# Layer 0's attention weights from image pairs (t, t+d): 17 differences instead of all 32 partners

## The chip, the cores and the metric

One core of one Trainium2 chip. The metric is the device time of one execution, in microseconds (us). Five runs of the kernel before the change lie between 3171.18 and 3187.57 us, median 3178.15 us. Everything is fp32.

## What is computed

The reference runs two layers on `x` of shape (4, 32, 128, 128). Layer 0 is a spectral-convolution attention over the 32 images of each of the 4 batches; layer 1 (pairwise attention over 1024 tokens and a mixture of experts) fills the rest of the time and is not touched. Cut to what matters, layer 0 is:

```
xn = inorm(group_norm(x))
k, q = fno_layer(xn, Kcw, Ksw, 64, 64), fno_layer(xn, Qcw, Qsw, 64, 64)   # 32 heads
v    = fno_layer(xn, Vcw, Vsw, 128, 128)
scores[b, n, t, s] = sum_k qf[b, n, t, k] * kf[b, n, s, k] / 64
p_attn = softmax(scores, axis=-1)             # 32 x 32 for each of 32 heads
av = p_attn @ v ; p = fno_layer(av, Pcw, Psw) ; norms, a two-layer fno, residuals
```

Keys and queries are spectral layers of one image each, so a score is a weighted sum, over the kept frequencies, of products of the two images' Fourier coefficients: for each head n, `w_re[mode, n]` times Re(X_t X_s*) and `w_im[mode, n]` times Im(X_t X_s*). The real part is the same for (t, s) and (s, t), the imaginary part changes sign.

## The kernel before, in words

**Spectra.** `spectra_of_images` turns the 32 images of a batch into `xx[p, t, y]`: 128 partitions are 64 row frequencies, real parts in the lower half, imaginary parts in the upper half; y counts column frequencies. ACT then copies the 17 kept column frequencies into `xm[p, 2*17, t]` (L457, two copies of 128x544 that turn t and y around): plane yy is the spectrum, plane 17+yy the spectrum with its halves turned and signed, so that a product of the two gives the imaginary part.

**Attention weights.** `attention_weights(b, front)` runs once per batch, four times in all, and is the only large piece that the change touches. Its steps in order:

- ACT copies the 17 planes into `xp` in PSUM (L495), so that DVE reads one operand from PSUM.
- PE sums the frequencies above 17, which all heads share, in `so[t, s]` (32x32; 15 pairs of L503, then L504); DVE spreads it on a diagonal as `sod` (32x1024, L506).
- For each of the 17 planes yy there are two outer products over t and s, each 128x1024: `pa` (real part) on DVE, `pb` (imaginary part) on DVE for every third plane (L522) and on POOL for the others (L524): 22 on DVE and 12 on POOL. PE contracts each over its 128 partitions, with `w_re` or `w_im` as stationary 128x32, in two halves of 512 columns (L528): four products per plane, one on each quarter of the 128 PSUM partitions of `sp`. A fp32 matmul shows as two records.
- ACT copies `sp` (128x512) to `spt` (L536). PE adds four terms into `sc` (64 x 32 x 16: two halves of t on partitions): `qk` by `sod` (L540) and `halves` by `spt` (L547), each for two halves.
- Softmax: DVE maximum (L558), DVE difference (L559), ACT Exp (L560), DVE sum (L562), reciprocal (L563), DVE product (L564). The result `ph` goes out to DRAM and comes back as `pr` in another layout (L572, L577).

**Buffers.** `sod`, `pa`, `pb`, `ph`, and later the `u` tiles share one tag `pr` with six buffers. `xp`, `so`, `sc`, and later the tiles `y1` and `xw`, share the PSUM tag `wide` with two buffers.

**What runs around it.** In layer 0 the order of each engine's work is decided by the framework's scheduler; each engine then runs its own list in order. For batch 0 the stage stands alone, with some setup on DVE behind it (L649 to L684). For batches 1 to 3 it overlaps the end of the batch before: ACT scales 32 images (L999), POOL adds them in four pieces (L1006), and after the stage PE and DVE run `back` (L297, L308) and the last residual (L1010). The next batch begins with `cm` (L703), and with `po` (L778), the products of `pr` with `u = xb*gb` (L773 on POOL, L775 on DVE).

Of the kernel before, what the change touches and what calls it, by code (L numbers as in the profile page):

```python
# [7 lines left out]
F32 = mybir.dt.float32  # L8
AF = mybir.ActivationFunctionType
ALU = mybir.AluOpType  # L10
# [3 lines left out]
P = 128  # L14
# [21 lines left out]
def _constants():  # L36

    w = np.arange(P)
    kx = np.concatenate([np.arange(32), np.arange(-32, 0)])
    ky = np.arange(KY)  # L40
    th = 2 * np.pi / P
    c, s = np.cos(th * np.outer(w, kx)), np.sin(th * np.outer(w, kx))
    rows = np.concatenate([c, -s], 1)
    inv_rows = np.concatenate([c.T, -s.T], 0)
    angle = th * np.outer(w, ky)
    cc, cs = np.cos(angle), np.sin(angle)

    cols1 = np.concatenate([cc[:, 32:33], cs, cc], 1) / NPIX
    cols2 = np.concatenate([0 * cc[:, :1], -cc, cs], 1) / NPIX
    along_c = np.concatenate([cc[:, 1:], cs[:, 1:], -cs[:, 1:]], 1) / NPIX  # L50
    twice = np.where(ky == 0, 1.0, 2.0)[:, None]
    re, im = twice * cc.T, -twice * cs.T
    inv_cols = np.concatenate([re, im], 0)
    back = np.tile(2 * np.concatenate([cc.T[1:], cs.T[1:]], 1), (4, 1))
    p = np.arange(P)
    same = (p[:, None] % 32 == np.arange(32)[None, :]).astype(np.float64)
    block = (p[:, None] // 32 == np.arange(4)[None, :]).astype(np.float64)

    eye = np.eye(32)
    comb = np.zeros((4, 32, 3, 32))  # L60
    comb[0, :, 0], comb[3, :, 0] = eye, -eye
    comb[1, :, 1], comb[2, :, 1] = eye, eye
    comb[:, :, 2] = -comb[:, :, 0]
    halves = np.concatenate([np.eye(64), np.eye(64)], 0)

    group = (p[:, None] // 4 == p[None, :] // 4) / (4.0 * NPIX / C * T)
    of_group = p[:, None] // 4 == np.arange(32)[None, :]
    by_p = np.concatenate(
        [rows, inv_rows, cols1, cols2, same, block, comb.reshape(P, 96), halves, group, of_group / 4]
        + [along_c, back],  # L70
        1,
    )
    return by_p.astype(np.float32), inv_cols.astype(np.float32)
# [35 lines left out]
def layer0(  # L109
# [37 lines left out]
    inv = columns(128)  # L147
    cols1, cols2 = columns(NX), columns(NX)
    same, block = columns(32), columns(4)
    comb, halves, group, of_group = columns(96), columns(64), columns(P), columns(32)  # L150
    cos_c, sin_c, minus_sin_c = columns(NY), columns(NY), columns(NY)
    cos_back, sin_back = columns(P), columns(P)
    par = const.tile([P, NSMALL], F32, name="par")
    nc.sync.dma_start(out=par, in_=small_row.partition_broadcast(P))
    ident = const.tile([P, P], F32, name="ident")
    make_identity(nc, ident)
    mean_w = const.tile([P, P], F32, name="mean_w")
    nc.vector.memset(mean_w, 0.5 / P)
    one_of_8 = const.tile([P, 39], F32, name="one_of_8")
    nc.vector.memset(one_of_8, 0.0)  # L160
    nc.vector.memset(one_of_8[:, 7:8], 1.0)
# [41 lines left out]

    def inv_std(name, var, n=T):

        ve, r, t = (one(f"{name}{k}", n) for k in ("_ve", "", "_t"))
        nc.vector.tensor_scalar(ve, var, 1e-5, None, ALU.add)
        nc.scalar.activation(r, ve, AF.Ln)
        nc.scalar.activation(r, r, AF.Exp, scale=-0.5)
        nc.vector.tensor_mul(t, r, r)  # L210
        nc.vector.tensor_mul(t, t, ve)
        nc.vector.tensor_scalar(t, t, -0.5, 1.5, ALU.mult, ALU.add)
        nc.vector.tensor_mul(r, r, t)
        return r, ve

    def stats(name, st):
# [9 lines left out]
        )  # L226
        nc.vector.tensor_tensor(pk[:, 1], pk[:, 1], sq[:, :, 1], ALU.add)
        m = ps.tile([P, 2, T], F32, name="m", tag="wide")
        nc.tensor.matmul(m, mean_w, pk, start=True, stop=True)
        mean, var = per_image(f"{name}_mean"), per_image(f"{name}_var")  # L230
        nc.vector.tensor_copy(mean, m[:, 0])
        nc.vector.tensor_mul(var, mean, mean)
        nc.vector.tensor_tensor(var, m[:, 1], var, ALU.subtract)

        x0 = ps.tile([P, 2, T], F32, name="x0", tag="wide")
        nc.tensor.matmul(x0[:, 0], rows, pk[:, 0], start=True, stop=True)
# [181 lines left out]
    def spectra_of_images(b, xt, normed):  # L418
# [33 lines left out]
        nc.vector.memset(xx[96:97, :, 0], 0.0)  # L452


        xm = modes.tile([P, 2 * KA, T], F32, name=f"xm_{b}", tag="xm")
        for k, y0 in enumerate((1 + KY, 1)):
            nc.scalar.copy(  # L457
                xm[:, k * KA : (k + 1) * KA], xx[:, :, y0 : y0 + KA].rearrange("p t y -> p y t")
            )
        return xx, xm, xd  # L460

    def value_weights():
        t1, t2 = (prep.tile([NH, KX, KA], F32, name=f"v{n}", tag=f"t{n}") for n in (1, 2))
# [7 lines left out]
        for ri, (b, d, op) in enumerate(  # L471
# [9 lines left out]
            for k in range(2):  # L481
# [2 lines left out]
                    in_=gd[ri, 16 * k : 16 * k + 16].unsqueeze(0).to_broadcast([8, 16, NM]),  # L484
                )

    def attention_weights(b, front):

        xx, xm, _ = front
        xs = per_image("xs")  # L490
        nc.vector.tensor_copy(xs, xx[:, :, 0])

        xp = ps.tile([P, KA, T], F32, name="xp", tag="wide")
        for y0, n in ((0, 16), (16, 1)):
            nc.scalar.copy(xp[:, y0 : y0 + n], xm[:, y0 : y0 + n])  # L495


        tt = [P, T, T]
        so = ps.tile([T, T], F32, name="so", tag="wide")
        xh = per_image("xh")  # L500
        nc.vector.tensor_scalar(xh, xs, 0.5, None, ALU.mult)
        for yy in range(KA, 32):
            nc.tensor.matmul(so, xx[:, :, 1 + KY + yy], xx[:, :, 1 + KY + yy], start=yy == KA, stop=False)  # L503
        nc.tensor.matmul(so, xh, xs, start=False, stop=True)  # L504
        sod = grp.tile([T, T, T], F32, name="sod", tag="pr", bufs=6)
        nc.vector.tensor_tensor(  # L506
            sod,
            ident[:T, :T].unsqueeze(2).to_broadcast([T, T, T]),
            so.unsqueeze(1).to_broadcast([T, T, T]),
            ALU.mult,  # L510
        )

        sp = ps.tile([P, T, 16], F32, name="sp", tag="b")
        for yy in range(KA):
            xs_p = xp[:, yy].unsqueeze(2).to_broadcast(tt)
            xs_s = xm[:, yy].unsqueeze(2).to_broadcast(tt)
            pa = grp.tile(tt, F32, name="pa", tag="pr", bufs=6)
            pb = grp.tile(tt, F32, name="pb", tag="pr", bufs=6)
            for k, t in enumerate((pa, pb)):
                other = xm[:, k * KA + yy].unsqueeze(1).to_broadcast(tt)  # L520
                if k == 0 or yy % 3 == 2:
                    nc.vector.tensor_tensor(t, xs_p, other, ALU.mult)  # L522
                else:
                    nc.gpsimd.tensor_tensor(t, xs_s, other, ALU.mult)  # L524
            for j, (wt, pp, h) in enumerate(
                (w, p, h) for w, p in ((w_re, pa), (w_im, pb)) for h in range(2)
            ):
                nc.tensor.matmul(  # L528
                    sp[32 * j : 32 * j + 32],
                    wt[:, yy],  # L530
                    pp[:, :, 16 * h : 16 * h + 16],
                    start=yy == 0,
                    stop=yy == KA - 1,
                )
        spt = grp.tile([P, T, 16], F32, name="spt", tag="v", bufs=3)
        nc.scalar.copy(spt, sp)  # L536
        nn = [2 * NH, T, 16]
        sc = ps.tile(nn, F32, name="sc", tag="wide")
        for h in range(2):
            nc.tensor.matmul(  # L540
                sc[32 * h : 32 * h + 32],
                qk,
                sod[:, :, 16 * h : 16 * h + 16],
                start=True,
                stop=False,
            )
            nc.tensor.matmul(  # L547
                sc[32 * h : 32 * h + 32],
                halves[:, 32 * h : 32 * h + 32],
                spt,  # L550
                start=False,
                stop=True,
            )


        ph = grp.tile(nn, F32, name="ph", tag="pr", bufs=6)
        mx = small.tile([2 * NH, 16], F32, name="mx", tag="mx")
        nc.vector.tensor_reduce(mx, sc.rearrange("n s t -> n t s"), AX.X, ALU.max)  # L558
        nc.vector.tensor_tensor(ph, sc, mx.unsqueeze(1).to_broadcast(nn), ALU.subtract)  # L559
        nc.scalar.activation(ph, ph, AF.Exp)  # L560
        sm = small.tile([2 * NH, 16], F32, name="sm", tag="mx")
        nc.vector.tensor_reduce(sm, ph.rearrange("n s t -> n t s"), AX.X, ALU.add)  # L562
        nc.vector.reciprocal(sm, sm)  # L563
        nc.vector.tensor_tensor(ph, ph, sm.unsqueeze(1).to_broadcast(nn), ALU.mult)  # L564

        prd = dram.tile([2, T, 16, T], F32, name=f"prd_{b}")
        pr = big.tile([P, 4, 2, T], F32, name=f"pr_{b}", tag="prob")
        for k in range(2):
            for h in range(2):
                eng = nc.scalar if h else nc.sync  # L570
                p0 = 32 * h + 16 * k
                eng.dma_start(  # L572
                    out=prd[k, :, :, 16 * h : 16 * h + 16].rearrange("s n t -> n s t"),
                    in_=ph[p0 : p0 + 16],
                )
            eng = nc.scalar if k else nc.sync
            eng.dma_start(  # L577
                out=pr[:, :, k], in_=prd[k].rearrange("(i s) n t -> (s n) i t", i=4)
            )
        return ph, pr  # L580
# [1065 lines left out]
```

## Time and profile before

| | |
|---|---|
| median of 5 runs | 3178.15 us |
| the profiled execution's own time | 3182.88 us |
| its span, first to last instruction | 3181.2 us |
| PE / DVE / ACT / POOL busy, share of the span | 92% / 72% / 73% / 66% |
| mean granted TensorE clock | 0.956 |
| layer 0 | about the first 1100 us; layer 1 begins to overlap it near the end |

The four attention stages, in us from the span's start:

| batch | first product (L522) | last contraction ends (L528) | `ph` ready (L564) | first `po` (L778) |
|---|---|---|---|---|
| 0 | 72.37 | 99.45 | 110.77 | 115.91 |
| 1 | 311.79 | 345.28 | 353.15 | 375.45 |
| 2 | 570.65 | 604.26 | 612.13 | 633.43 |
| 3 | 830.60 | 864.08 | 871.95 | 890.03 |

How to read the views: a group's row gives engine, operation, what it writes and reads, shape and count, then the mean time of one. In the chain of waits each piece is start, length and what ran, followed back from the last instruction to what released it; "issue" is time in which the profile shows no wait. In a table of stretches, PEclk is the granted TensorE clock as a share of full speed.

### The profile page before, as it was taken

Reading aid. Unit: us, or ns where it says so; the run is one execution under the profiler, and the core shown is the slowest. Engines: PE = TensorE matmul, PEld = TensorE weight load, DVE = VectorE, ACT = ScalarE, POOL = GpSimd, SP = SyncE. Lnnn points to the kernel's source line nnn. Section 1 sums busy time; section 2 is a strip of 40 time slices with the busy share of each in tenths; the row PEclk is TensorE's granted clock in tenths of the full one; section 3 lists DMA queues with packets and bytes.
Section 4 is the critical chain, followed back from the end, with each engine's and each line's share of the span. In section 5 each row is a group of like instructions: output and inputs, shape, how many; then the busy total and the mean of one; then the engine's idle time right before and its main releaser. Section 6 shows DMA issues by size and latency. Waiting matters only on the chain.

```text
span 3181.2 us, 53099 instructions
## 1 busy us (share of the span) xinstructions
PE 2920.5 (92%) x19634; PEld 1431.4 (45%) x19634; DVE 2290.3 (72%) x5035; ACT 2310.2 (73%) x3138; POOL 2102.3 (66%) x1831
## 2 busy tenths in 40 slices
PE   7889798798888789999999999999999999999997
PEld 5366266355446444443344444444444444444443
DVE  5876667667677466777666868866778777777887
ACT  2334244254353589998999999998999999999992
POOL 0721540460461389878788797889878889888773
PEclk6998899899898799999999999999999999999998
DMA  6301310230140211010111010011010011101000
GB/s 140 108 22 30 89 56 8 55 112 1 31 129 2 61 27 31 8 30 7 31 37 24 14 24 14 8 41 31 21 34 4 14 37 24 37 1 31 14 14 14
DMA packets 152309, 112.77 MB, mean 35 GB/s; under 512 B 36879, under 2 KB 140658, under 8 KB 151442
## 3 DMA queue, kind: packets, MB, share of 16 engines
q1 hardware_dynamic: 136209, 103.61, 12.2%
q10 hardware_dynamic: 15840, 5.77, 0.8%
q8 instruction: 155, 2.54, 0.3%
q14 instruction: 105, 0.85, 0.1%
HBM read 68.37 MB, written 20.00 MB: 28 GB/s over the span
## 4 chain that ended last, share of the span: by engine, by line
PE 59%; POOL 13%; DVE 9%; ACT 9%; issue 8%; DMA 1%; ACTq 0%; POOLq 0%; DVEq 0%; SPq 0%
PE d L1446 18%; PE po L1465 10%; PE px L1352 6%; ACT r L1496 4%; PE po L778 4%; PE n L1446 3%; POOL e L1504 3%; POOL e L1505 3%; PE pz L248 2%; POOL kx L1111 2%; PE four L308 2%; ACT e L1512 2%; PE px L871 1%; PE sk L742 1%; DVE r L1501 1%
## 5 line engine op out<-in xcount | busy, mean ns | idle before, releaser
L1501 DVE TENSOR_TENSOR r<-n,r 128x1024 f32<-128x1024 f32 (+1 forms) x1056 | 961.3, 952 | 479.3 <-PE n L1446 394.4
L1504 POOL TENSOR_TENSOR e<-r 128x512 f32<-128x512 f32 x528 | 673.0, 1275 | 268.1 <-DVE r L1501 267.7
L1496 ACT ACTIVATE r<-d 128x1024 f32<-128x1024 f32 (+1 forms) x1056 | 792.8, 802 | 67.6 <-PE n L1446 56.5
L1508 ACT ACTIVATE r<-r 128x1536 f32<-128x1536 f32 x528 | 783.6, 1484 | 16.8
L1505 POOL TENSOR_TENSOR e<-e,r 128x512 f32<-128x512 f32 x528 | 671.3, 1271 | 41.4
L1446 PE MATMUL d<-qe,ke 32*128 32x512 f32 (+3 forms) x2304 | 605.6, 602 | 39.8 <-ACT r L1496 36.6
L1465 PE MATMUL po<-e,kx 128*128 128x512 f32 (+3 forms) x1152 | 594.4, 605 | 15.6 <-POOL e L1517 15.6
L1446 PE MATMUL n<-qe,ke 32*128 32x512 f32 (+3 forms) x2304 | 606.0, 601 | 0.0
L1446 PE MATMUL n<-qf,kf 32*128 32x512 f32 (+3 forms) x2304 | 552.5, 554 | 0.0
L1446 PE MATMUL d<-qf,kf 32*128 32x512 f32 (+3 forms) x2304 | 550.2, 553 | 0.0
L1356 DVE SCALAR_TENSOR_TENSOR xc<-px,wgt,xc 128x128 f32<-128x128 f32 x1024 | 358.0, 350 | 42.2 <-PE px L1352 9.7
L1512 ACT ACTIVATE e<-e 128x512 f32<-128x512 f32 x528 | 325.8, 617 | 66.1 <-POOL e L1505 65.5
L1465 PEld LDWEIGHTS po<-e,kx 128*128 128x128 f32 x1152 | 175.4, 188 | 392.9 <-issue 307.1
L1446 PEld LDWEIGHTS d<-qe,ke 32*128 32x128 f32 x2304 | 176.3, 183 | 359.5 <-ACT r L1496 339.6
L773 POOL TENSOR_TENSOR u<-xb,gb 128x858 f32<-128x858 f32 (+1 forms) x120 | 232.7, 1963 | 141.4 <-PE po L778 129.5
L1446 PEld LDWEIGHTS d<-qf,kf 32*128 32x128 f32 x2304 | 220.1, 186 | 176.3 <-issue 163.9
L1352 PE MATMUL px<-we,x2t 128*128 128x512 f32 x512 | 264.0, 601 | 6.8 <-DVE xc L1356 5.9
L775 DVE TENSOR_TENSOR u<-xw,gb 128x858 f32<-128x858 f32 (+1 forms) x200 | 206.3, 1081 | 59.1 <-PE po L778 46.9
L885 POOL TENSOR_TENSOR spec<-part,part 128x512 f32<-128x512 f32 x16 | 24.8, 1550 | 322.6 <-ACT z L188 75.2
L1446 PEld LDWEIGHTS n<-qf,kf 32*128 32x128 f32 x2304 | 228.1, 185 | 19.2 <-issue 11.6
L778 PE MATMUL po<-u,pr 128*32 128x429 f32 (+1 forms) x1280 | 191.5, 549 | 25.8 <-DVE u L775 11.2
L524 POOL TENSOR_TENSOR pb<-xm 128x1024 f32<-128x1024 f32 x48 | 90.7, 1914 | 159.7 <-ACT xm L457 153.3
(388 smaller groups left out, 3937.1 us busy)
## 6 DMA issues: line engine op xcount, KB each, us to landing
xb<-xd SPq DMA_DIRECT2D x128, 214.5 KB
xc<-x SPq DMA_DIRECT2D x29, 512.0 KB
x<-x SPq DMA_DIRECT2D x16, 512.0 KB
qf<-qe SPq DMA_DIRECT2D x64, 128.0 KB
out<-xc SPq DMA_DIRECT2D x15, 512.0 KB
xb<-xd SPq DMA_DIRECT2D x32, 198.0 KB
gb<-gd SPq DMA_DIRECT2D x4, 1056.0 KB
x<-in_x SPq DMA_DIRECT2D x8, 512.0 KB
```

Of the source, the lines that this page charges most:

```text
L773: nc.gpsimd.tensor_tensor(u, xb, gk, ALU.mult)
L778: nc.tensor.matmul(po[32 * j : 32 * j + 32], pr[:, i, k], u[:, r], start=i == 0 and k == 0, stop=i == 3 and k == 1,)
L1352: nc.tensor.matmul(px, x2t[:, k * P : (k + 1) * P], we[:, e0 : e0 + 4], start=True, stop=True)
L1356: nc.vector.scalar_tensor_tensor(xc[:, k], px[:, e], wgt[:, k, e0 + e : e0 + e + 1], xc[:, k], ALU.mult, ALU.add)
L1446: nc.tensor.matmul(o, k, q, start=turn == 0 or g > 0, stop=turn == 1 or g > 0)
L1465: nc.tensor.matmul(sums[c, h][:, q0 : q0 + c1 - c0], kx[:, jb], e[:, c0:c1], start=jb == 0, stop=is_last and q0 > 2 * P, skip_group_check= ...
L1496: nc.scalar.activation(r[:, g], d, AF.Ln, scale=1.0 / DSCALE)
L1501: nc.vector.tensor_tensor(r[:, g], part, r[:, g], ALU.mult)
L1504: nc.gpsimd.tensor_tensor(e, r[:, 1], r[:, 2], ALU.add)
L1505: nc.gpsimd.tensor_tensor(e, e, r[:, 0], ALU.add)
L1508: nc.scalar.activation(r, r, AF.Exp, scale=-1.0)
L1512: nc.scalar.activation(e, e, AF.Exp)
```

## The change

Each plane now forms products only for pairs (t, t+d), d = 0 to 16 (index taken modulo 32): 544 columns instead of 1024. `xe` holds the spectrum with its first 16 images repeated, so that a window of 17 that slides by one image is the second operand. The other half of the pairs comes out of the same sums, by sign (`plus_minus`) and by order of reading (`steps`). Even and odd planes are summed on different partition quarters of `sp`; the column d = 0 is summed apart in `sp0`. The softmax is laid out by d, its exponentials are written twice, and the last product reads them along a diagonal.

```diff
-        xm = modes.tile([P, 2 * KA, T], F32, name=f"xm_{b}", tag="xm")
-        for k, y0 in enumerate((1 + KY, 1)):
-            nc.scalar.copy(
-                xm[:, k * KA : (k + 1) * KA], xx[:, :, y0 : y0 + KA].rearrange("p t y -> p y t")
-            )
+        xe = modes.tile([P, KA, T + T // 2], F32, name=f"xe_{b}", tag="xe")
+        xm = modes.tile([P, KA, T], F32, name=f"xm_{b}", tag="xm")
+        for dst, y0, n in ((xe[:, :, :T], 1 + KY, T), (xe[:, :, T:], 1 + KY, T // 2), (xm, 1, T)):
+            nc.scalar.copy(dst, xx[:, :n, y0 : y0 + KA].rearrange("p t y -> p y t"))
...
+    def steps(a, *dims):
+        return bass.AP(tensor=a.tensor, offset=a.offset, ap=[a.ap[0], *dims])
...
+            x_y = xx[:, :, 1 + KY + yy]
+            nc.tensor.matmul(
+                so, x_y, x_y.unsqueeze(1).to_broadcast(twice), start=yy == KA, stop=False
+            )
...
         for yy in range(KA):
-            xs_p = xp[:, yy].unsqueeze(2).to_broadcast(tt)
-            xs_s = xm[:, yy].unsqueeze(2).to_broadcast(tt)
+            row = xp[:, yy // 9, yy % 9 * (T + half) :]
             pa = grp.tile(tt, F32, name="pa", tag="pr", bufs=6)
             pb = grp.tile(tt, F32, name="pb", tag="pr", bufs=6)
             for k, t in enumerate((pa, pb)):
-                other = xm[:, k * KA + yy].unsqueeze(1).to_broadcast(tt)
-                if k == 0 or yy % 3 == 2:
-                    nc.vector.tensor_tensor(t, xs_p, other, ALU.mult)
+                other = (xm[:, yy] if k else xe[:, yy, :T]).unsqueeze(2).to_broadcast(tt)
+                if k == 0 or yy % 2 == 1:
+                    nc.vector.tensor_tensor(t, steps(row, [1, T], [1, nd]), other, ALU.mult)
                 else:
-                    nc.gpsimd.tensor_tensor(t, xs_s, other, ALU.mult)
...
+            for k, (wt, pp) in enumerate(((w_re, pa), (w_im, pb))):
+                r = 32 * (2 * k + yy % 2)
+                nc.tensor.matmul(sp[r : r + 32], wt[:, yy], pp[:, :, 1:], **turn)
+            r = 32 * (yy % 2)
+            nc.tensor.matmul(sp0[r : r + 32], w_re[:, yy], pa[:, :, 0], **turn)
-        spt = grp.tile([P, T, 16], F32, name="spt", tag="v", bufs=3)
-        nc.scalar.copy(spt, sp)
+        spt = grp.tile([P, 2, T, half], F32, name="spt", tag="pr", bufs=6)
+        nc.scalar.copy(spt, sp.unsqueeze(1).to_broadcast([P, 2, T, half]))
+        spt0 = small.tile([2 * NH, T], F32, name="spt0", tag="ym")
+        nc.vector.tensor_copy(spt0, sp0)
...
+            nc.tensor.matmul(o[:, :, 1:nd], both_plus, spt[:, 0, i], start=False, stop=False)
+            nc.tensor.matmul(
+                o[:, :, nd:], plus_minus, steps(first, [half, half], [half - 1, half - 1]), start=False, stop=False
             )
+            nc.tensor.matmul(o[:, :, 0], both_plus[: 2 * NH], spt0[:, i], start=False, stop=True)
...
+        less = grp.tile(nn, F32, name="less", tag="v", bufs=3)
+        nc.vector.tensor_tensor(less, sc, mx.unsqueeze(2).to_broadcast(nn), ALU.subtract)
+        ex = grp.tile([2 * NH, half, 2, T], F32, name="ex", tag="pr", bufs=6)
+        nc.scalar.activation(ex, less.unsqueeze(2).to_broadcast([2 * NH, half, 2, T]), AF.Exp)
+        nc.vector.tensor_reduce(sm, ex[:, :, 0], AX.X, ALU.add)
+        nc.vector.reciprocal(sm, sm)
...
+        for h in range(2):
+            r = slice(32 * h, 32 * h + 32)
+            first = ex.rearrange("n t r d -> n (t r d)")[r, T - half * h :]
+            nc.vector.tensor_tensor(
+                ph[r],
+                steps(first, [1, T], [2 * T - 1, half]),
+                sm[r].unsqueeze(1).to_broadcast([32, T, half]),
+                ALU.mult,
+            )
```

In this diff `tt` is `[P, T, 17]` after the change, the matmuls into `sp` were four of 512 columns per plane, and `sc` still begins with `qk` by `sod` for each half. Smaller edits: the constant `halves` is replaced by `both_plus` and `plus_minus`; the constant `mean_w` goes, and its factor 0.5/P moves into the two DVE instructions that read the sums in `stats`; the scratch tile of `inv_std` is shared under one tag.

In the program built from it, each stage has 25 products of 128x544 on DVE and 9 on POOL; on POOL the four additions (L1021 now) stand behind the first, second, fourth and fifth of the nine.

## The prediction

> **What bounds the kernel now.** I read the page first: PE is busy 92% of the span, but that is an average, and the change lies in four stages of about 40 us each in layer 0. So I went to the table of stretches for the stage of batch 0 (first row below) and of batch 3 (the other two), where the columns are length, then busy time of PE, weight loads, DVE, ACT and POOL, then the granted clock:
>
> ```profile
> 72.00:99.50 27.50, 25.54 (x138) 4.95 (x138) 27.03 (x25) 1.32 (x5) 23.43 (x13) 0.87 0.48 107
> 829.00:864.00 35.00, 25.59 (x144) 5.33 (x142) 26.93 (x23) 13.54 (x35) 32.90 (x17) 0.79 0.06 16
> 864.00:872.00 8.00, 6.86 (x72) 3.79 (x70) 3.35 (x6) 1.21 (x2) 2.96 (x2) 1.00 0.01 2
> ```
>
> In batch 0 DVE is full (27.03 of 27.5). In batch 3 POOL is (32.90 of 35), since it also does the four additions of L1006. The chain of waits for batch 3 says the same, and then shows the tail, in which one thing runs at a time:
>
> ```profile
> 829.65 3.77 POOL pb L524 x2
> 833.42 2.32 POOL x L1006
> ...
> 848.57 2.37 POOL x L1006
> 850.94 0.18 POOL pb L524
> ...
> 864.76 1.04 PE sc L547 x2
> 865.81 0.97 PE sc L540 x2
> 866.78 0.99 PE sc L547 x2
> 867.79 0.69 DVE mx L558
> 868.51 0.69 DVE ph L559
> 869.29 0.64 ACT ph L560
> 869.95 1.01 DVE sm L562
> 870.99 0.26 DVE sm L563
> 871.26 0.69 DVE ph L564
> 872.00 1.12 PE cm L703 x2
> ```
>
> After `ph` the chain goes on through `back` and `cm` without a pause, so the stage's length passes to the total nearly one for one. The prices come from the groups by form and the timeline:
>
> ```profile
> L522 DVE TENSOR_TENSOR pa<-xp,xm 128x1024 f32<-128x1024 f32 x68 | 80.2, 1216 | 18.5 <-PE sp L528 18.0
> L615 DVE TENSOR_TENSOR w_im<-w_im,wt 128x544 f32<-128x544 f32 x1 | 0.7, 715 | 0.0
> L562 DVE TENSOR_REDUCE sm<-ph 64x16 f32<-64x512 f32 x4 | 4.0, 1000 | 2.3 <-ACT ph L560 2.3
> 840.75 1.07 PE L528 MATMUL sp<-pb,w_im 128*32 128x512 f32 x2 [2.38 <-POOL pb L524]
> 846.80 0.62 PE L528 MATMUL sp<-pb,w_im 128*32 128x512 f32 x2 [1.64 <-POOL pb L524]
> ```
>
> Here a DVE product of 544 columns has a row of its own shape, a strided read of 512 values costs 1000 ns against 0.68 us for the maximum (L558), and the same matmul takes 1.07 or 0.62 us by the granted clock.
>
> **DVE products.** In the timeline of batch 0 three products start within 3.47 us, 1.13 us apart; four of them (one period of three planes) take 4.52 us. A product of 544 lasts 0.715 instead of 1.216 us, so they will be 0.63 apart. 25 x 0.63 = 15.8 us for a batch, against 22 x 1.13 = 24.9. The operand is a sliding window, a form that the trace does not show: below, 0.715; above, the strided row's price (1.000 - 0.15)/512 = 1.66 ns a value, 1.05 us. The window's inner step is one value, as in L615, so I take 0.715.
>
> **POOL products.** 1.912 us for 1024 (L524) and 0.298 us for 64 in rows of 8 (L1347) give 1.68 ns a value: 1.10 us for 544. Rows of 17 get no surcharge because rows of 8 show none; the bounds are 1.10 and 1.91 (nothing saved). 9 x 1.10 = 9.9 us against 12 x 1.91 = 22.9.
>
> **PE.** Two matmuls of 512 columns and one of 32 per plane replace four of 512. Four ran side by side on the four quarters, so a plane took two passes of 0.43 us; now two planes can share that time. PE needs about 1 us per pair of planes (2 at the halved clock), DVE 1.89: PE is not the limit. Buffers are nearly one: `sod` holds one of six, as before, and a tile occupies its buffer for 0.71 + 0.12 + 1.05 + 0.12 us, some 2.0 to 2.6. Four tiles over five buffers are 1.7 us per pair, under 1.89 by little.
>
> **Start.** `so` gets 64 columns instead of 32. Its 30 records are 71 ns apart now; at the clock of that moment (0.50 in the row of 828.00 to 832.40) 512 columns take 0.853 us, so 64 take 107 ns: +1.1 us, and `sod` and the first product of batch 0 start at 73.45. ACT's third copy of 272 values (0.68 us by L457's 1.17 for 544) stands ahead of the last spectrum in ACT's list, where ACT idles 5.5 us before L457; without that cover it costs 0.7 us. The copies into `xp` get 0.3 us longer.
>
> **Batch 0.** Products: 73.45 + 15.8 + last contraction 1.1 + 0.6 for handing over = 91, against 99.45. Behind the products DVE has its setup rows, 97.89 to 105.52 = 7.6 us, and only then the maximum; `sc` is ready at about the same time, so its growth is hidden there. The maximum moves from 105.5 to about 97. Two `u` products (L775, 1.03 us each) that DVE ran inside the softmax now stand behind it, which pays for the longer softmax. Batch 0: **-8**.
>
> **Batches 1 to 3.** POOL's list in batch 3: first product 829.65 to 830.75; the first addition needs eight ACT images and cannot start before 833.6 (833.4 now, plus 0.25 for `xp`); then four additions of 2.37 and eight products of 1.10 without a wait, ending at 851.9. DVE can be only five tiles ahead: six are left when the tenth plane is released at about 849.9, 3.8 us, then 1.1 for PE and about 1 for handing over: 856, against 864.08. That is -8; I give back 1 for matmuls at the halved clock in POOL's pauses: -7.
>
> The tail grows. `spt` 0.585 to 1.01 (L1496, 128x1024 from PSUM): +0.4. `sc` gets, per half, 240 columns (0.5 us from L547's 0.98 for 512) and 16 columns with another row shape (0.3, as L504's two records of 32 columns): +1.6. Exp 0.63 to 1.05 (L326, 128x1024): +0.4. The sum is now contiguous: -0.3. Two last products instead of one, read along a diagonal, 0.68 to 1.0 each: +0.6 to +1.3, taken as 1.0. Together +3.1 (2.5 to 4). `spt0` is a small DVE copy beside ACT's. Net **-4** per batch, -12 for three.
>
> **At nothing:** `stats` and `inv_std` keep their instructions, with equal durations (0.18 to 0.24 us rows), and `mean_w` was 0.1 us of startup. The engines' lists outside the stages are unchanged except that the scheduler interleaves `cm`, `po` and `skips` differently at the start of batch 3: a few us either way.
>
> **Sum:** -8 - 12 = -20, so the profiled execution goes from 3182.88 to 3163; against the median, which lies 4.7 lower, 3158.
>
> **A rule against it.** The granted clock falls when PE starves: in the row at 840.75 the matmuls are at 1.07 us after an idle 2.38 us, and back at 0.60 from 844.13. The Trainium skill, TensorE: Matmul & The Clock Gate, section "The HAM clock gate", says that the clock is halved after an idle window of about 3.4 us and restored after a busy one. The change thins PE out, and batches 1 to 3 get a pause of some 3 us behind POOL's first addition. By the rule the clock would be back before `sc`, as the stretch from 847.6 has work every 2 us, and the sum stays at -20; were it not, the second rival holds.
>
> **The rivals.**
> - *POOL saves nothing* (1.9 us a product, chance 0.10). The profile speaks against it with L1347. POOL then ends at 859 and PE at 860.6: -3.5 and +3 in batches 1 to 3; batch 0 -6: total -8, 3170.
> - *The halved clock stays through the tail* (0.12), the slower side. PE busy half the time does not win the clock back; 0.79 now in a denser stage speaks for it. Contraction ends 5.7 earlier instead of 8, `sc` takes 9 us for 3 (+6), the rest of the tail +1.5, and the matmuls behind it +1.7: +3.5 per batch. Batch 0: 96.5 + 1 + 9, so the maximum at 106.5, +1. Total +11, 3189. It decides if the granted clock from the last contraction to `cm` is under 0.7.
> - *The gain is absorbed* (0.08): something else, the `pr` round trip or `xb`, sets the start of `po`. In batches 1 to 3 `pr` is issued 15 us before `po`, so only the residual could. Total within 9, say 3176.
>
> **How the numbers follow.** The forecast has 0.70: -20, with -10 to -34 from the tail, the DVE price and the shuffled list of batch 3: 3144 to 3168. A change of 0.3% (9.5 us) is about what the runs can tell from none. Faster: 0.64 of the forecast, 0.04 of POOL, 0.02 of the absorbed, 0.70. Same: 0.06, 0.06, 0.04 and 0.01 of the clock: 0.17. Slower: 0.11 of the clock and 0.02: 0.13. From 3140 to 3178 the range holds the forecast, POOL and most of the absorbed case, over 0.8.
>
> **What would show it.** Right: L534 rows of 0.71 us, 0.63 apart; POOL rows of 1.1; last contraction 26 us after the first product in batch 3 and 18 in batch 0; tail 11 instead of 8 us. Wrong: DVE rows near 1.05, POOL rows near 1.9, a clock under 0.7 in the tail, or stages that shorten while the first `po` stays put.

## The result, and the profile after

The changed kernel takes 3175.87 us (median of 37 runs, 3168.79 to 3189.92) beside 3179.46 for the kernel before (median of 64): a ratio of 0.9988, 95% interval 0.9981 to 0.9995. The sign was right and the size was not: 3.6 us came off where 20 were forecast.

The profiled execution after has a span of 3173.7 us and a mean granted clock of 0.953. The prices of single instructions were right, as the groups by form show (columns: busy, mean ns | idle of the engine before them, and what ended it):

```profile
L534 DVE TENSOR_TENSOR pa<-xp,xe 128x544 f32<-128x544 f32 x68 | 48.2, 716 | 24.3 <-PE sp L540 22.7 <-PE sp L542 1.4
L536 POOL TENSOR_TENSOR pb<-xe,xm 128x544 f32<-128x544 f32 x36 | 40.6, 1127 | 178.7 <-ACT xm L458 149.5 <-PE sp L540 23.9 <-PE sp L542 5.2
L540 PE MATMUL sp<-pb,w_im 128*32 128x512 f32 x136 | 52.6, 720 | 26.6 <-POOL pb L536 26.6
```

DVE's product takes 716 ns and POOL's 1127 ns. The news is in the last columns: in the four stages together DVE stands idle for some 24 us for PE, POOL for some 29 us for PE, and PE for 26.6 us for POOL. All three wait for one another. The table of stretches says the same (the products of batch 0, those of batch 3, the tail of batch 3, and a stretch behind it; columns as before):

```profile
72.00:94.60 22.60, 19.36 (x104) 4.88 (x104) 18.91 (x39) 0.00 (x0) 9.01 (x8) 0.90 0.46 97
822.50:849.00 26.50, 18.21 (x106) 5.51 (x108) 16.57 (x26) 10.77 (x29) 18.16 (x12) 0.81 0.05 17
849.00:859.80 10.80, 9.04 (x80) 5.06 (x80) 4.58 (x7) 2.03 (x2) 2.00 (x1) 0.93 0.01 2
858.30:868.50 10.20, 9.75 (x14) 2.70 (x14) 4.99 (x12) 1.09 (x2) 2.00 (x1) 0.50 0.22 26
```

Before, one engine was full in each product stage (DVE in batch 0, POOL in batch 3). Now none is: 19.36 us of 22.6 on PE and 18.91 on DVE in batch 0, and 18.2, 16.6 and 18.2 of 26.5 on PE, DVE and POOL in batch 3. The timeline of batch 0 shows how. First POOL alone, then DVE alone:

```profile
83.16 1.13 POOL L536 TENSOR_TENSOR pb<-xe,xm 128x544 f32<-128x544 f32 x1 [1.18 <-PE sp L540]
85.47 1.13 POOL L536 TENSOR_TENSOR pb<-xe,xm 128x544 f32<-128x544 f32 x1 [1.18 <-PE sp L540]
```

```profile
83.16 0.72 DVE L534 TENSOR_TENSOR pa<-xp,xe 128x544 f32<-128x544 f32 x1 [0.32 <-PE sp L540]
83.80 0.71 DVE L534 TENSOR_TENSOR pb<-xp,xm 128x544 f32<-128x544 f32 x1
84.43 0.71 DVE L534 TENSOR_TENSOR pa<-xp,xe 128x544 f32<-128x544 f32 x1
85.47 0.72 DVE L534 TENSOR_TENSOR pa<-xp,xe 128x544 f32<-128x544 f32 x1 [0.32 <-PE sp L540]
```

A pair of planes takes 2.31 us. POOL works for 1.13 us and waits for 1.18; DVE makes three products and waits for 0.32. Both start again at the same instant, 83.16 and 85.47, when a contraction on PE releases buffers.

The chain of waits for batch 3, from the last contraction on:

```profile
848.33 0.65 PE sp L540
848.98 1.00 ACT spt L544
...
855.56 1.06 ACT ex L566
...
857.64 1.07 DVE ph L574
858.71 0.04 issue
858.75 2.07 PE cm L718 x2
860.82 2.00 PE four L308 x2
862.83 2.00 PE cm L718 x2
864.83 3.71 PE four L308 x4
```

The tail is 10.86 us long, 7.87 before. Behind it two `cm` records take 2.07 us, against 1.12 before: the clock is 0.50 there (the stretch from 858.30 above).

By parts, in us, with the mean of two profiles each for before and after (the runs of the unchanged kernels below gave the second ones), and the run with `sod` apart, which the next section explains:

| part | before | after | `sod` apart |
|---|---|---|---|
| batch 0, `ph` ready at | 108.9 | 106.0 | 100.4 |
| batch 0, `ph` to first `po` | 5.2 | 6.4 | 5.75 |
| batches 1 to 3, `so` to `ph`, sum | 133.9 | 126.2 | 113.1 |
| batches 1 to 3, `ph` to first `po`, sum | 60.6 | 65.7 | 66.7 |
| three gaps, first `po` to the next `so` | 577.2 | 579.5 | 579.3 |
| from batch 3's first `po` to the end | 2290.7 | 2290.2 | 2290.2 |
| span | 3176.5 | 3174.0 | 3155.4 |

Read from top to bottom, the change shortened the stages by 10.6 us (2.9 and 7.7), not by 20, and of these 6.3 were lost again between `ph` and `po` and 2.3 in the gaps. Batch 0 has to be read with care, since it doesn't begin at the same time in every execution: `so` starts at 68.9 and 56.8 us in the two profiles before, at 67.2 and 69.1 after, and at 66.8 with `sod` apart. Counted from `so`, its `ph` came after 41.8 us in the first profile before, and after 38.3 and 37.4 us in those of the changed kernel.

### The profile page after: what moved, and what is told of

The parts are those of the page before. It is cut to its first block, busy times and chain, and to the rows that moved or that the text cites. A ratio compares the mean times of both kernels' runs of the same rounds, so it can differ in the third digit from the quotient of the medians.

```text
span 3173.7 us, 52863 instructions
## 1 busy us (share of the span) xinstructions
PE 2916.7 (92%) x19530; PEld 1444.2 (46%) x19530; DVE 2257.8 (71%) x5054; ACT 2318.9 (73%) x3142; POOL 2055.2 (65%) x1819
## 4 chain that ended last, share of the span: by engine, by line
PE 60%; POOL 14%; ACT 10%; DVE 8%; issue 7%; DMA 1%; POOLq 0%; DVEq 0%; ACTq 0%; SPq 0%
PE d L1461 18%; PE po L1480 10%; PE px L1367 5%; ACT r L1511 5%; PE po L793 4%; POOL e L1520 3%; POOL e L1519 3%; PE n L1461 3%; PE pz L248 2%; PE four L308 2%; ACT e L1527 2%; POOL kx L1126 2%; DVE r L1516 2%; PE px L886 2%; PE sk L757 1%
## 5 line engine op out<-in xcount | busy, mean ns | idle before, releaser
L1527 ACT ACTIVATE e<-e 128x512 f32<-128x512 f32 x528 | 325.8, 617 | 67.2 <-POOL e L1520 66.2
L793 PE MATMUL po<-u,pr 128*32 128x429 f32 (+1 forms) x1280 | 194.9, 555 | 26.5 <-DVE u L790 14.4
L1461 PEld LDWEIGHTS n<-qe,ke 32*128 32x128 f32 x2304 | 177.5, 183 | 9.3 <-DVE r L1516 0.9
```

Source lines behind the costliest of these rows:

```text
L793: nc.tensor.matmul(po[32 * j : 32 * j + 32], pr[:, i, k], u[:, r], start=i == 0 and k == 0, stop=i == 3 and k == 1,)
L1461: nc.tensor.matmul(o, k, q, start=turn == 0 or g > 0, stop=turn == 1 or g > 0)
L1527: nc.scalar.activation(e, e, AF.Exp)
```

## Experiments

**Both kernels again**, without an edit.

> The kernel before, unchanged, to read the granted clock of each of its runs. Over the 37 runs of the changed kernel, time falls by 2.0 us for each 0.001 of mean granted clock (correlation -0.89), and their mean clock is 0.953. Theory C (the stages got shorter as forecast in kind, but PE loses its full clock more often and gives the gain back): the mean clock of these runs is higher, 0.956 to 0.958, and at equal clock the changed kernel is 9 to 14 us faster. Rival A (the gain is absorbed by another wait behind the stages): the same mean clock, 0.953, and no gap at equal clock beyond 4 us. Ratio to itself 1.000.

> The changed kernel, unchanged, on the same chip and in the same rounds. Theory C: mean clock 0.953 and 3 to 5 us faster than before; its profile shows the clock at 0.5 between the softmax and the first po of batches 1 to 3 for some 8 us each, as in its first profile. Rival A: the same time, with the clock no different from before.

Measured: 3176.64 us for the kernel before (ratio 0.9997, interval 0.9984 to 1.0011), 3177.11 for the changed one (0.999, 0.9975 to 1.0006). So the change is worth a few us at most. The mean granted clock over 12 runs each was 0.9586 and 0.9528. Within the 37 runs of the changed kernel the time falls by 2.0 us for each +0.001 of clock (correlation -0.89). That is a correlation: it doesn't say which way it works. By this price the gap of 0.006 in clock is worth some 12 us, so Theory C had both the clocks and the gap at equal clock right, and Rival A had not. Whether the lower clock is the cause of the lost time is another question; the runs with added matmuls below raise the clock, and no gain in time shows.

**`sod` apart: a sixth buffer for the products.**

```diff
-        sod = grp.tile([T, T, T], F32, name="sod", tag="pr", bufs=6)
+        sod = big.tile([T, T, T], F32, name="sod", tag="rs")
```

> The changed kernel with sod in the buffer of rs, which is idle then, so that pa and pb have six buffers instead of five. Theory B (the products run in lock-step: a POOL product, then its contraction, then the buffer it frees, 2.31 us per pair of planes, where DVE alone would need 1.89): the period falls to about 1.9, the stage of batch 0 from 22.4 to about 19 us, the other three by 1 to 3 us each; total -5 to -12 us against the changed kernel. Rival (DVE and POOL were the limit anyway): period and total within 2 us of the changed kernel.

Measured: 3159.04 us, ratio 0.9937 (0.9918 to 0.9955), 20 us under the kernel before and 17 to 18 under the changed one (3175.87 and 3177.11). From the first product to the last contraction: 18.21 us in batch 0 (22.39 after), and 22.95, 23.58 and 22.97 in the others (25.40, 26.26, 26.40). From the timeline of batch 0, POOL alone:

```profile
76.59 1.13 POOL L536 TENSOR_TENSOR pb<-xe,xm 128x544 f32<-128x544 f32 x1 [0.43 <-PE sp L540]
78.49 1.13 POOL L536 TENSOR_TENSOR pb<-xe,xm 128x544 f32<-128x544 f32 x1 [0.76 <-PE sp L540]
80.38 1.13 POOL L536 TENSOR_TENSOR pb<-xe,xm 128x544 f32<-128x544 f32 x1 [0.76 <-PE sp L540]
```

and the stretch of batch 0's products:

```profile
70.40:88.60 18.20, 17.58 (x107) 7.53 (x105) 18.19 (x39) 0.01 (x1) 9.25 (x9) 1.00 0.36 58
```

The period is 1.89 us (78.49 to 80.38), that is three DVE products, and DVE is full again, 18.19 of 18.2 us. The edit did more than that, since the scheduler ordered the lists anew: the product that makes `sod` now stands behind the first `pa` instead of ahead of it, so that the first product starts 3.6 to 3.8 us after `so`, not 5.0; and in batches 1 to 3 POOL's four additions stand behind the first, third, fourth and sixth of its nine products.

**`sod` apart, but five buffers again.** To part the buffer from the order, the edit above with `tag="pr", bufs=5` wherever it said 6. The order on POOL and the early first `pa` are those of the run above.

> The changed kernel with sod in the storage of rs, as in the run before that gained 20 us, but with the ring pr cut from six buffers to five, so that the products have the same five buffers as in the changed kernel, while sod still lies apart and its product still comes behind the first pa. Theory B (the sixth buffer made the gain): pa start to sp end goes back to 22 us in batch 0 and 25 to 26 in the others, period of a pair of planes about 2.3 us in batch 0; time 3172 to 3178, with 1 us per batch kept for the earlier first product. Rival D (the gain came from the order, sod's product and the sc matmul no longer standing ahead of the first products): pa start to sp end stays 18 in batch 0 and 23 in the others, time 3157 to 3162.

Measured: 3189.81 us, ratio 1.0038 (1.0026 to 1.005). The products are back at 21.04 us in batch 0 (18.21 with six buffers) and take 28.49, 27.64 and 27.61 in the others, even longer than in the changed kernel, while the start stays at 3.6 to 3.8. From the timeline, POOL alone:

```profile
72.27 1.13 POOL L536 TENSOR_TENSOR pb<-xe,xm 128x544 f32<-128x544 f32 x1 [1.18 <-PE sp L540]
74.58 1.13 POOL L536 TENSOR_TENSOR pb<-xe,xm 128x544 f32<-128x544 f32 x1 [1.18 <-PE sp L540]
```

The period of 2.31 us and the wait of 1.18 are the changed kernel's own. So the buffer shortened the products, and the order only the start. In batches 1 to 3 the earlier start bought nothing by itself: from the start of `so` to the last contraction this run takes 31.4 to 32.2 us, the changed kernel 30.5 to 31.5, and six buffers 26.6 to 27.4. The total is no price for the buffer alone, and the forecast of 3172 to 3178 missed: the smaller ring serves the `u` tiles too, and the three gaps from `po` to the next `so` grew from 579.5 to 589.6 us.

**`sod` apart in the kernel before**, the same one-line edit.

> The kernel before with only sod moved to the storage of rs, so that its products have six buffers. Theory B says that the kernel before is held by DVE's own list of products (a pair of planes takes what DVE's instructions take), so a sixth buffer gives at most the start: pa before sod, 1.2 us per batch less, minus nothing behind it: 3172 to 3178, ratio 0.998 to 1.000. If the move alone is worth what it was worth in the changed kernel, 3160 (ratio 0.994), then the 20 us do not belong to the half products at all.

Measured: 3187.86 us, ratio 1.0029 (1.0015 to 1.0042). No gain, so the 20 us belong to the half products *with* the sixth buffer. That it is slower was not expected. Its first product comes 3.4 to 3.6 us after `so`, as without the edit. The products of the profiled execution took 28.0 us in batch 0 (27.1 and 26.5 without the edit) and 32.7 in the others (32.7 to 33.6), but that execution (3176.03) was one of the fastest of its kernel, and the mean clock over the 12 runs was 0.9524 beside 0.9594 for the kernel before. What costs the 9 us stays open.

**No products on POOL**, five buffers as in the changed kernel.

```diff
-                if k == 0 or yy % 2 == 1:
+                if True:
```

> The changed kernel with all 34 products on DVE and none on POOL; sod stays in the ring, so five buffers. Theory B (five buffers fall into lock-step only because POOL holds one for 1.13 us and starts when one comes free): DVE runs its products at its own pace, 34 x 0.63 = 21.5 us, so pa start to sp end 22 to 23 us in every batch, where the changed kernel has 22.4, 25.4, 26.3 and 26.4; batch 0 the same, batches 1 to 3 together 10 us less, if DVE's other work of that stage doesn't fill the gain; time 3164 to 3172. Rival E (five buffers are too few for any engine): waits for PE stay in the rows of L534, pa start to sp end 25 or more, 3175 to 3182.

Measured: 3170.83 us, ratio 0.9976 (0.9964 to 0.9989). Products 22.64, 23.66, 23.46 and 23.46 us. The groups by form:

```profile
L534 DVE TENSOR_TENSOR pa<-xp,xe 128x544 f32<-128x544 f32 x68 | 48.3, 710 | 0.0
L534 DVE TENSOR_TENSOR pb<-xp,xm 128x544 f32<-128x544 f32 x68 | 48.4, 711 | 2.3 <-PE sp L540 2.2
```

With five buffers and nine more products per batch DVE hardly waits for PE (2.2 us in all, 24.1 in the changed kernel). Five buffers are thus enough for a producer that takes 0.63 us a product; they are too few when one of them holds a slow one. Taking POOL away shortened batches 1 to 3 from `so` to `ph` by 7.8 us together (118.4 beside 126.2). The total is no worse; that it is better isn't shown, since the interval of the ratio overlaps the changed kernel's (0.9981 to 0.9995).

**No products on POOL and `sod` apart**, both edits.

> The same, all products on DVE, and sod in the storage of rs, so six buffers. DVE's own pace of 21.5 us is then the bound: pa start to sp end 22 in batch 0 (3.5 more than with POOL) and 22 to 23 in the others (as with POOL, 23). Theory B: time 3157 to 3165, that is 0 to 4 above the run with POOL and six buffers (3159), and 3 to 8 below the run with five buffers and DVE alone, which is the earlier first product (1.2 us per batch).

Measured: 3169.3 us, ratio 0.9976 (0.9964 to 0.9988): a miss, 4 to 12 above what was expected. The products took 24.76 us in batch 0, 3 more than expected, and 23.78 in the others, 1 more. Beside the run with five buffers and no POOL (23.46 to 23.66 in batches 1 to 3) the sixth buffer no longer shortens them. Above all, batch 0's first `po` came at 113.86 us, against 106.2 with POOL. ACT alone, in the timeline of batch 0:

```profile
94.43 0.52 ACT L782 COPY xw<-xb 128x429 f32<-128x429 f32 x1 [33.93 <-DMA xb<-xd]
94.88 1.01 ACT L544 COPY spt<-sp 128x1024 f32<-128x1024 f32 x1
```

The scheduler put a copy of `xw` ahead of `spt` in ACT's list, and that copy waited for the transfer of `xb` until 94.43, while the last contraction had ended at 85.3. The kernel before has the same order: in its second profile `spt` ran at 95.49, with the contraction done at 86.7. The changed kernel and the run with `sod` apart have `spt` first, but there such copies stand ahead of the Exp. With `sod` apart the last of them waited for `xb` until 95.75 us, and the Exp came at 96.20; with three matmuls added as well (below) the last contraction of batch 0 ended at 78.6 us, ten earlier, and `ph` came at 99.9, no earlier to speak of. Batch 0 therefore gains from earlier products only up to the landing of `xb`.

**A tail longer by 3 us, in the kernel before.**

```diff
+        for _ in range(4):
+            nc.vector.tensor_tensor(ph, ph, ones[: 2 * NH, :16].unsqueeze(1).to_broadcast(nn), ALU.mult)
```

> The kernel before with four products more of ph by ones (64 partitions by 512, about 0.7 us each) ahead of the DMAs of the weights, about 2.9 us per batch: the price of a tail longer by as much as the change's (3.0). If a longer tail is paid once: 12 us more, 3188 to 3192, ratio 1.003 to 1.004. If work behind the stage hides part of it: 3178 to 3185. If the halved clock behind a longer wait adds to it (Theory C: 2 to 5 us per batch more in ph to po): 3195 to 3205.

Measured: 3192.43 us, ratio 1.0057 (1.004 to 1.0074), 15 us more. The tail grew from 7.87 to 10.74 us in batches 1 and 2 and 11.23 in batch 3. The longer tail is paid in full: nothing hides it. The interval, 13 to 24 us, allows something beyond the 12, and doesn't settle it.

**Work for PE in the tail.** In the changed kernel, behind the Exp, with a result that nobody reads:

```diff
+        wm = ps.tile([P, 512], F32, name="wm", tag="a")
+        for _ in range(3):
+            nc.tensor.matmul(wm, ones[: 2 * NH], less.rearrange("n t r -> n (t r)"), start=True, stop=True)
```

> The changed kernel with three extra matmuls of 64x128 by 512 columns in every batch, which read the differences of the softmax and write a tile that nobody reads, so that PE has work while ACT and DVE finish the softmax. Theory C: the clock stays at 1.0 behind the softmax in more of the batches, back runs at full clock, total -4 to -12 us against the changed kernel, mean clock 0.954 to 0.957. If the clock loss behind the softmax does not come from PE's idle time there, the three matmuls only cost: 0 to +5 us.

> The changed kernel with sod in the storage of rs and, besides, three more 64x128 by 512 matmuls of less behind the Exp, whose result nobody reads: the two edits that were run alone. If they add: 3159 less 2 to 4, so 3155 to 3157. If the granted clock behind the stage is worth 4 us in each of batches 1 to 3, as the changed kernel's batch 3 suggested: 3147 to 3150. If the free running of the clock's windows decides and not the load in the tail: 3157 to 3161.

> The changed kernel with sod in the storage of rs and five matmuls of less instead of three behind the Exp. Of the profiles so far, batch 3's time from ph to the first po stands at about 18.0 us and 0.45 us for each us of halved clock in it (0.0 us: 18.08; 3.3: 19.03; 8.9: 22.60; 24.4: 28.96). Theory C (PE's idle time in the tail halves the clock behind it): halved clock in ph to po falls from 8 to 9 us to under 4 in batches 1 to 3, 2 us per batch less, 3150 to 3154, mean granted clock 0.962 or more. Rival F (the clock's windows fall as they will, load in the tail does little): 8 us on average as before, 3156 to 3161, mean clock 0.955 to 0.958.

Measured: with three matmuls 3173.77 us (0.9984, 0.9969 to 0.9999); with three and `sod` apart 3154.27 (0.993, 0.9913 to 0.9947); with five and `sod` apart 3157.51 (0.9932, 0.9914 to 0.9949). The intervals overlap those without the matmuls (0.9988 and 0.9937): no gain is shown. The mean clock did rise, to 0.956 alone and 0.962 with `sod` apart (0.953 and 0.9565 without). In the profile with five, batch 3 went from `ph` to `po` in 26.4 us. The clock fell to 0.50 at 846.39, while the added matmuls were running, and these (ten records, 7.32 us from 844.75 on) and 32 records of `y` stood ahead of `cm` in PE's list, so that `cm` began only 5.9 us after `ph`. In batches 1 to 3 of this profile, the slowest of its six executions, the halved clock between `ph` and `po` lasted 1.9, 19.3 and 11.1 us, where Theory C wanted under 4 and Rival F some 8. So neither expectation holds whole: the mean clock rose as Theory C said, and the time stayed where Rival F put it.

The best versions are those with `sod` apart, six buffers and some products on POOL: 3154 to 3159 us, with or without the added matmuls.

## Why the prediction was right or wrong

**DVE products, POOL products, the tail: right.** DVE 0.716 us (0.715 forecast) and 0.63 apart; the sliding window has no surcharge. POOL 1.127 (1.10). The tail +3.0 us (+3.1) in batches 1 to 3, and the experiment in the kernel before shows that it is paid.

**The step that failed: "Buffers are nearly one".** It took the average time that a tile holds its buffer, 2.0 to 2.6 us, times four tiles, over five buffers: 1.7 us per pair, "under 1.89 by little", so DVE would set the pace. The upper end of its own range, 2.6, gives 2.08 us, above 1.89, so the sum didn't carry the conclusion even as an average. The runs show 2.31 us with five buffers and 1.89 with six. An average over buffers holds only if each is refilled at once by whoever is ready. Here the order in which the ring (the buffers of tag `pr`) is passed on decides: POOL's product of 1.13 us can't start before PE has released a buffer, PE can't finish the pair before POOL's product is there, and that contraction releases the next buffer. The two add up in series, 1.13 + 1.18 = 2.31. The sixth buffer lets POOL start one step ahead; without POOL, five suffice. That is 13.1 us over batches 1 to 3 (126.2 to 113.1 in the table). For batch 0 the table has 5.6 us, but the earlier first product (some 1.3 us), the moment at which `so` begins and the landing of `xb` are in that figure too; the products alone, 21.04 and 18.21 us with five and six buffers, put the buffer's share there at some 2.8 us.

**Start: mis-sized.** +1.1 us was forecast and +1.5 measured (`so` to first product 3.5 us before, 5.0 after). The 30 records of `so` took 3.67 us instead of 2.14. With `sod` apart they take as long, and yet the first product comes only 0.2 to 0.3 us later than before: the 64 columns cost something because the product that makes `sod` stood ahead of the first `pa`.

**Batch 0: -8 forecast, -2.9 measured, -8.5 with six buffers.** Last contraction 22.4 us after the first product (21.6 in the second profile), where 18 was named as the sign of being right; with `sod` apart it was 18.2. The -2.9 leans on a profile before whose `so` began 12 us early; counted from `so`, the first profile before gives -4.

**Batches 1 to 3: -4 each forecast, -2.6 measured up to `ph`, -6.9 with six buffers.** The sign named, the contraction 26 us after the first product, came true (25.4 to 26.5), for the wrong reason: POOL's list with its four additions was taken as the bound, "without a wait". In the changed kernel POOL does wait, four times for a buffer in batch 3 (2.05 us, then three times 1.18). With six buffers the list is what the prediction took it for: in batch 3 POOL works from the first addition, 811.08, to 828.04 without a pause, and ends 22.4 us after its first product, as forecast (829.65 to 851.9). The contraction comes 1.8 us behind that end, where 4.1 were forecast, so 23 us after the first product on DVE.

**The interleaving behind batch 3, "a few us either way": +4.5.** From `ph` to `po` it went from 18.08 to 22.60 us, the same in both profiles of either kernel. PE's order changed and the clock as well. The halved clock is the part that the profiles support: the kernel before with `sod` apart keeps its old order (one `cm` pair, four, `y`), has 6.8 us of halved clock there, and takes 21.31 us. Its chain of waits:

```profile
864.11 2.07 PE cm L703 x2
866.18 3.71 PE four L308 x4
869.89 1.11 PE y L297 x6
871.00 1.07 PE four L308 x2
```

That is 3.2 us more for 6.8 us of halved clock, or 0.47 us for each; by that price the changed kernel's 8.9 us give 4.2 of the 4.5. It is a price from one profile: batch 3 of the run with the longer tail had 3.1 us of halved clock and took 18.09 us all the same, and no profile has the changed kernel's order at full clock. How much of the 4.5 is order stays open. Why its tails are followed by 7 to 9 us of halved clock in every profile, and those of the kernel before by 0 to 9, isn't shown: the longer tail in the kernel before had 7.2, 14.0 and 3.1.

**The rivals.** *POOL saves nothing* is out by L536. *The halved clock stays through the tail* named its test, a clock under 0.7 from the last contraction to `cm`: 0.93, so it fell, though the clock is 0.50 directly behind. *The gain is absorbed* named the right time (3176) and in the main a wrong mechanism: the stages themselves shortened too little, by 10.6 us, and 6.3 more were lost between `ph` and `po`, where the prediction let the stage's length pass "nearly one for one". That the run with six buffers comes out at the forecast time is partly luck: its stages gain 29 us, not 20, and some 8 are given back behind them.

The Trainium skill, "TensorE: Matmul & The Clock Gate", section "The HAM clock gate", speaks of free-running windows of about 3.4 us, and these profiles agree: the halved stretches here are 10.2 and 6.8 us long, three and two times 3.41. It gives an idle window as what halves the clock. Here the measurement differs: in the 3.41 us ahead of the halved stretch of batch 3, from 854.88 to 858.29, PE was busy for 2.35 us, with `y` matmuls whose weights are 32 rows, and the clock fell all the same.

Counted over such windows from 55 to 1000 us in the thirteen profiles here: at full clock, each of the 120 in which PE was busy for less than 40% was followed by a halved one, none of the 1737 with 95% or more was, and in between it went both ways. Of the 176 halved windows in which PE was busy for less than 80%, none was followed by a full one. The busy time of PE alone thus doesn't say which way a tail like these will go.

## What to carry to other kernels

When products get shorter, do the sum of the buffers again as a loop, not as an average: follow one buffer from its release through the slowest producer and the consumer to its next release, and compare that with the pace of the fast producer. If three engines each wait for the other two and none is full, look for a tile that sits in the ring without being part of the loop, and move it. And let an experiment change one thing: the edit that moved `sod` also moved other instructions in the lists, and only the run with five buffers told which of them counted.

## What the runs showed of the hardware

A PE that is busy two thirds of the time with small matmuls still lost its clock (2.35 of 3.41 us, then 0.50 for 10.2 us). Matmuls added to keep it up didn't always do so: in one profile the clock fell 1.6 us after they had begun, in a window with PE busy for 3.01 of 3.41 us, and most of them ran at 0.50. And a DVE product that reads a sliding window costs what a plain one does (716 and 715 ns for 544 columns), while the same ring with one slower producer in it cost 0.42 us a pair of planes.
